# A selective scan behind two convolution blocks: softplus summed in PSUM, one odd product in five moved from GpSimd to VectorE, and the background work cut and paced anew

## The chip, the cores and the metric

One Trainium2 chip, one of its NeuronCores. Five engines run their own instruction streams in order and wait for each other by semaphores: TensorE (PE; its weight loads are PEld), VectorE (DVE), ScalarE (ACT), GpSimd (POOL) and SyncE (SP), which here only issues DMAs. SBUF is the on-chip memory of 128 partitions; PSUM holds what TensorE writes, eight banks of 128 x 512 fp32. The metric is the device time of one execution in microseconds.

## The reference

An image batch x of 16 x 64 x 64 x 96 (fp32) goes through two blocks, each with a group norm ahead and a residual. The first block upsamples by two in the Fourier domain, applies a 96-to-384 layer, a polynomial of second degree, a 384-to-96 layer, and low-passes back. The second is a selective scan in four directions, and the time goes there. Cut to what matters:

```
x = x + L0(gn(x))
x = x + L1(gn(x))
# inside L1, for each of 4 directions k, 192 channels d, 16 states n, 4096 places l:
delta = softplus(dts + bias)
h     = exp(delta * A) * h + (delta * u) * B
y     = sum over n of h * C   (+ u * Ds)
# then: layer norm of the four directions' sum, times silu(z), out projection
```

Softplus is computed as max(s, 0) + ln(1 + e) with e = exp(-|s|), and the rounding error of 1 + e is taken off: minus ((1 + e) - 1 - e).

## The kernel before, in words

`front(mi)` makes everything of image mi that comes ahead of the scan: its two norms, the first block (upsampling matmuls `u_ps`, `xu_ps`, the layers `h_ps`, `o_ps`, the way back `d_ps`, `e_ps`), then the 3 x 3 convolution `c_ps` with silu, with results written to DRAM (`xs`, `z`, `x1`). `finish(mi)` sums the directions after the scan, norms, gates and projects. `project` makes, for each step of 1024 places, the rows B and C and for three channel groups v delta = softplus(s) and dtu = delta * u, in pieces of 128 x 512, and writes them to DRAM. All three are Python generators; each `yield` ends a slice of work.

The scan is the main loop. It runs over 16 images, 8 steps per image (four chunks of 1024 places forward, four backward, two directions in each), 6 blocks of channels and 4 groups j of states: 3,072 positions n. A position works on 128 lanes (32 channels x 4 states) in two halves e = 1 ("odd") and e = 0 ("even"), each 128 x 1024:

- GpSimd `drive(n)`: b = dtu * B for both halves at once (128 x 2048, L725). `b` has three buffers, all in SBUF.
- ScalarE `decay(n, e)`: da = exp(delta * A) (L719). `da` lies in PSUM, two buffers, one for each half.
- VectorE `recur(n, e)`: the scan itself (L734 forward, L736 backward). The odd scan writes over its half of b, the even one over da in PSUM.
- ScalarE `keep(n, e)`: the last column, as the start of the next chunk (L742).
- The product of h with C: the odd half in place on GpSimd (L863, b and ct in SBUF), the even half on VectorE (L873, da in PSUM times ct in SBUF, into b).
- TensorE `read_out(n)`: sums over the states into the PSUM tile y (L758). `store` copies y out after each fourth position.

The order is written out by hand and is the order of every engine's stream. In position n: odd scan, `read_out(n - 1)`, a slot, `keep` and `decay(n + 1)` of the odd half, odd product, `drive(n + 2)`, even scan, a slot, even product, `keep` and `decay(n + 1)` of the even half, a slot. `drive(n + 2)` writes the buffer that `read_out(n - 1)` reads; the next odd product on GpSimd needs the next odd scan and the `keep` that reads its result.

In each `slot()` one slice of `project` for the next step is taken, and one of the background: `front` of the next image until it is done, then `finish` of the image before. `Background.slot` hands out SLICES = 404 slices in POS = 576 slots of an image, so about 0.70 per slot, whatever a slice holds.

Large transfers of `front` and `finish` (the image in, the way back `s`, `x1`, the turned `xs` out, `ycol` in: 7 per image of 0.75 to 2 MB) are issued on ScalarE's queue; all others, those for the scan among them, on SP's.

Of the kernel before, what the change touches and what calls it, by code (L numbers as in the profile page):

```python
# [51 lines left out]
C = 96  # L52
# [19 lines left out]
SLICES = 404  # L72
PSLICES = 60


@with_exitstack
def tile_two_blocks(
    ctx: ExitStack, tc: tile.TileContext,
    x, w1, w1t, b1, w2t, b2, coef, inpt, convw, convb, xpt, dtw, alog, dsk, onw, onb, opt,
# [31 lines left out]
    nc.gpsimd.memset(one_s, 1.0)  # L111
    eps_g = const.tile([128, 1], F32, name="eps_g")
# [79 lines left out]

    def norm(xt):
# [37 lines left out]
    def front(mi):  # L231

        x_c = x[mi].rearrange("h c w -> c h w")
# [7 lines left out]
        nc.scalar.dma_start(out=xt.rearrange("c (h w) -> c h w", w=HW), in_=x_c)  # L241
        for _ in range(4):
            yield
# [163 lines left out]
        for i, on in enumerate((slice(0, JS), slice(JS, HW))):  # L407
            nc.scalar.dma_start(out=s[i], in_=s_d[:, on, :])
        for _ in range(8):
            yield  # L410
        x1 = xt
# [19 lines left out]
        nc.scalar.dma_start(out=made["x1"], in_=x1)  # L431
# [13 lines left out]
        for i, n, tiles, both in ((0, 128, 8, 0), (1, 64, 4, 4)):  # L445
            col = b16.tile([128, tiles * TB], F32, name="col", tag="b16")
            parts = [(n * k, t0) for k, t0 in enumerate((0, both)[:128 // n])]
            turned = None

            def turn(t, row, z):  # L450
# [4 lines left out]
                for p, t0 in parts:  # L455
                    cols = slice(TB * (t + t0), TB * (t + t0) + TB)
                    nc.sync.dma_start(out=made["xs"][2 * i, 0:n, cols], in_=row[p:p + n])
                    nc.sync.dma_start(out=made["z"][128 * i:128 * i + n, cols], in_=z[p:p + n])

            for t in range(tiles):  # L460
                c_ps = bank([128, 8, HW], "c_ps")
                for tap in range(9):
                    dy, dx = divmod(tap, 3)
                    for p, t0 in parts:
# [8 lines left out]
                    if tap % 3 == 2 and tap < 8:  # L473
                        yield
                z_ps = bank([128, 8, HW], "z_ps")
                for p, t0 in parts:
# [5 lines left out]
                yield  # L482
# [5 lines left out]
                yield  # L488
            turn(*turned)
            yield  # L490
            if i == 0:
                nc.scalar.dma_start(out=made["xs"][1], in_=col)
            else:
                for p, t0 in parts:
                    to = made["xs"][2, 64:128, :].rearrange("c (w h) -> c w h", h=HW)
                    for w0 in range(0, HW, 16):
# [4 lines left out]
                        yield  # L501

    def finish(mi):
# [3 lines left out]
        nc.scalar.dma_start(out=ycol[0], in_=y_d[1, 0:128, :])  # L507
        nc.scalar.dma_start(out=ycol[1], in_=y_d[1, 128:DI, :])
# [11 lines left out]
        for _ in range(6):  # L520
            yield
        tail = None
        for t in range(8):
# [7 lines left out]
            for ob, n in ((0, 128), (1, 64)):  # L531
# [11 lines left out]
                yield  # L543
# [12 lines left out]
                yield  # L556
# [5 lines left out]
            yield  # L562
# [5 lines left out]
            yield  # L568
# [6 lines left out]
            yield  # L575
# [4 lines left out]
            yield  # L580
# [10 lines left out]
        for _ in tail:  # L591
            yield
# [6 lines left out]
    def scan():  # L599


        with ExitStack() as es:
# [12 lines left out]
            def project(mi, pair, lc, out):  # L615
# [7 lines left out]
                for t in range(0, T, TB):  # L623
# [15 lines left out]
                    for i, v in enumerate((0, 2, 1)):  # L639
# [10 lines left out]
                        e = pj.tile([128, TB], F32, name="e")  # L650
                        d = pj.tile([128, TB], F32, name="d")
                        nc.scalar.activation(e, s, AF.Abs)
                        nc.scalar.activation(e, e, AF.Exp, scale=-1.0)
                        yield
                        nc.scalar.activation(d, e, AF.Ln, bias=one_s)  # L655
                        yield
                        nc.vector.scalar_tensor_tensor(d, s, 0.0, d, ALU.max, ALU.add)  # L657
                        yield
                        nc.scalar.activation(s, e, AF.Identity, bias=one_s)
                        yield  # L660
                        nc.vector.scalar_tensor_tensor(s, s, -1.0, e, ALU.add, ALU.subtract)
                        nc.vector.tensor_sub(s, d, s)
                        yield
# [3 lines left out]
                        yield  # L667
# [118 lines left out]
            class Background:  # L786


                def __init__(self, gen, slices, positions):
                    self.gen, self.slices, self.positions, self.at, self.n = gen, slices, positions, 0, 0  # L790

                def slot(self):
                    self.at += 1
                    if self.gen is not None and self.n * self.positions < self.at * self.slices:
                        self.n += 1
                        if next(self.gen, 0) == 0:
                            self.gen = None

                def drain(self):
                    while self.gen is not None:  # L800
                        self.n += 1
                        if next(self.gen, 0) == 0:
                            self.gen = None
# [15 lines left out]
            for n, (st, bi, j) in enumerate(units):  # L819
# [11 lines left out]
                if j == 0:  # L831
                    if bi == 0 and st + 1 < len(steps):
                        if steps[st + 1][0] > mi:
                            ahead_gen.drain()
                        step_gen = Background(project(*steps[st + 1], ctxs[st + 1]), PSLICES, 58)
# [20 lines left out]
                recur(n, 1, h)  # L856
                if n:
                    read_out(n - 1)
                slot()
                keep(n, 1, h)  # L860
# [142 lines left out]
```

## Time and profile before

| | us |
|---|---|
| median of 3 runs | 22,337.41 (22,315.87 to 22,346.83) |
| the profiled execution | 22,310.87, span 22,309.1 |
| GpSimd busy | 20,896.4 (94%) |
| VectorE busy | 19,837.0 (89%) |
| TensorE busy, granted clock 0.74 on average | 15,814.4 (71%) |
| ScalarE busy | 13,129.1 (59%) |
| DMA queue of SP, share of 16 engines | 54.6% |
| DMA queue of ScalarE | 3.0% |

The groups on VectorE that the change touches:

```
L657 DVE SCALAR_TENSOR_TENSOR d<-s,d 128x512 x768 | 521.8, 679
L661 DVE SCALAR_TENSOR_TENSOR s<-s,e 128x512 x768 | 521.9, 680
L662 DVE TENSOR_TENSOR s<-d,s 128x512 x768 | 534.4, 696
L666 DVE TENSOR_TENSOR dtu<-s,u 128x512 x768 | 516.6, 673
```

A row is read so: source line, engine, operation, what it writes and reads, shape, how often; then the busy time of all in us and the mean of one in ns. (The rows here are cut after that.) A wait is put down to the instruction that came last. Where two records of an engine overlap by a few hundredths of a microsecond, the distance from start to start is what one instruction really takes of the engine's time.

### The profile page before, as it was taken

Reading aid. Unit: us, or ns where it says so; the run is one execution under the profiler, and the core shown is the slowest. Engines: PE = TensorE matmul, PEld = TensorE weight load, DVE = VectorE, ACT = ScalarE, POOL = GpSimd, SP = SyncE. Lnnn points to the kernel's source line nnn. Section 1 sums busy time; section 2 is a strip of 40 time slices with the busy share of each in tenths; the row PEclk is TensorE's granted clock in tenths of the full one; section 3 lists DMA queues with packets and bytes.
Section 4 is the critical chain, followed back from the end, with each engine's and each line's share of the span. In section 5 each row is a group of like instructions: output and inputs, shape, how many; then the busy total and the mean of one; then the engine's idle time right before and its main releaser. Section 6 shows DMA issues by size and latency. Waiting matters only on the chain.

```text
span 22309.1 us, 261027 instructions
## 1 busy us (share of the span) xinstructions
PE 15814.4 (71%) x92844; PEld 6455.6 (29%) x92844; DVE 19837.0 (89%) x12829; ACT 13129.1 (59%) x20854; POOL 20896.4 (94%) x6152
## 2 busy tenths in 40 slices
PE   6675777767778677776777777677786777767745
PEld 4322323223232322323223232332323223232211
DVE  0999999899998999989899898999989999898996
ACT  3665655656556565565656556565565655656543
POOL 0999999999999999999999999999999999999997
PEclk7676777877778677686777878677786776867856
DMA  2555565655656556565655656556565665656654
GB/s 77 185 194 184 191 210 182 209 191 193 206 189 210 184 198 204 190 210 186 203 194 191 210 184 209 192 189 209 189 212 184 201 201 190 210 186 203 211 177 133
DMA packets 1915769, 4276.30 MB, mean 192 GB/s; under 512 B 543454, under 2 KB 642686, under 8 KB 1906206
## 3 DMA queue, kind: packets, MB, share of 16 engines
q1 hardware_dynamic: 1804702, 4086.06, 54.6%
q10 hardware_dynamic: 109760, 173.55, 3.0%
q8 instruction: 731, 11.98, 0.2%
q14 instruction: 576, 4.72, 0.1%
HBM read 3380.58 MB, written 878.18 MB: 191 GB/s over the span
## 4 chain that ended last, share of the span: by engine, by line
POOL 31%; issue 20%; DVE 20%; PE 15%; DMA 8%; ACT 5%; SPq 1%; POOLq 0%; ACTq 0%; DVEq 0%
POOL b L863 15%; POOL b L725 15%; DVE da L736 4%; DVE b L734 4%; DVE da L734 4%; DVE b L736 3%; DVE b L873 3%; PE y L758 2%; PE c_ps L466 2%; DMA u<-xs_d 2%; PE pp L633 2%; ACT da L719 2%; PE yc L535 1%; DMA ct<-rows 1%; PE oe_ps L578 1%
## 5 line engine op out<-in xcount | busy, mean ns | idle before, releaser
L725 POOL TENSOR_TENSOR b<-dtu,bt 128x2048 f32<-128x2048 f32 x3072 | 14000.3, 4557 | 578.3 <-DMA dtu<-dtu_d 531.9
L758 PE MATMUL y<-b,fold_s 128*32 128x256 f32 x49152 | 4865.1, 506 | 4962.9 <-DVE b L873 3489.3
L719 ACT ACTIVATE da<-delta,a_s 128x1024 f32<-128x1024 f32 x6144 | 6855.9, 1116 | 2487.3 <-DVE b L873 1350.0
L863 POOL TENSOR_TENSOR b<-b,ct 128x1024 f32<-128x1024 f32 x3072 | 7323.1, 2384 | 668.3 <-ACT new L742 591.3
L758 PEld LDWEIGHTS y<-b,fold_s 128*32 128x32 f32 x49152 | 1324.5, 127 | 8709.7 <-DVE b L873 4353.2
L873 DVE TENSOR_TENSOR b<-da,ct 128x1024 f32<-128x1024 f32 x3072 | 3750.4, 1221 | 75.1
L736 DVE TENSOR_TENSOR_SCAN b<-da,new,b 128x1024 f32<-128x1024 f32 x1152 | 2697.2, 2341 | 376.5 <-ACT new L742 223.5
L734 DVE TENSOR_TENSOR_SCAN b<-da,new,b 128x1024 f32<-128x1024 f32 x1152 | 2700.9, 2344 | 288.4 <-POOL b L725 283.4
L736 DVE TENSOR_TENSOR_SCAN da<-da,new,b 128x1024 f32<-128x1024 f32 x1152 | 2692.7, 2337 | 108.4 <-ACT da L719 108.4
L734 DVE TENSOR_TENSOR_SCAN da<-da,new,b 128x1024 f32<-128x1024 f32 x1152 | 2693.5, 2338 | 85.3 <-ACT da L719 85.3
L742 ACT COPY new<-da 128x1 f32<-128x1 f32 x2304 | 362.6, 157 | 3347.7 <-DVE b L873 3344.4
L466 PE MATMUL c_ps<-xgp,wtap_s 96*128 96x512 f32 (+1 forms) x4608 | 1676.9, 625 | 119.1 <-ACT row L484 114.5
L643 PE MATMUL s<-pr,dtw_s 128*128 128x512 f32 x1536 | 1202.3, 875 | 244.6 <-ACT delta L668 212.5
L358 PE MATMUL h_ps<-xu,w1t_s 96*128 96x500 f32 x1920 | 1316.4, 798 | 74.3 <-ACT hsq L341 32.8
L633 PE MATMUL pp<-u,xpt_s 128*128 128x512 f32 x1536 | 1061.8, 844 | 372.9 <-DMA u<-xs_d 359.8
L370 PE MATMUL o_ps<-w2c_s,hsq 128*100 128x96 f32 x9600 | 1222.0, 296 | 25.8 <-ACT new L742 15.1
L370 PEld LDWEIGHTS o_ps<-w2c_s,hsq 128*100 128x100 f32 x9600 | 1154.6, 208 | 284.9 <-issue 186.6
L742 ACT COPY new<-b 128x1 f32<-128x1 f32 x2304 | 429.9, 187 | 1058.2 <-DVE b L734 587.7
L657 DVE SCALAR_TENSOR_TENSOR d<-s,d 128x512 f32<-128x512 f32 x768 | 521.8, 679 | 555.6 <-ACT d L655 553.1
L736 DVE TENSOR_TENSOR_SCAN da<-da,b 128x1024 f32<-128x1024 f32 x384 | 876.5, 2282 | 133.5 <-ACT da L719 133.5
L734 DVE TENSOR_TENSOR_SCAN b<-da,b 128x1024 f32<-128x1024 f32 x384 | 876.2, 2282 | 99.3 <-POOL b L725 65.7
L736 DVE TENSOR_TENSOR_SCAN b<-da,b 128x1024 f32<-128x1024 f32 x384 | 876.5, 2283 | 69.8 <-POOL b L725 65.5
(120 smaller groups left out, 18395.2 us busy)
## 6 DMA issues: line engine op xcount, KB each, us to landing
dtu<-dtu_d SPq DMA_DIRECT2D x1536, 512.0 KB
delta<-delta_d SPq DMA_DIRECT2D x1536, 512.0 KB
bt<-rows SPq DMA_DIRECT2D x1024, 512.0 KB
ct<-rows SPq DMA_DIRECT2D x1024, 512.0 KB
u<-xs_d SPq DMA_DIRECT2D x896, 256.0 KB
dtu_d<-dtu SPq DMA_DIRECT2D x768, 256.0 KB
delta_d<-delta SPq DMA_DIRECT2D x768, 256.0 KB
xr<-in_x SPq DMA_DIRECT2D x768, 128.0 KB
```

What stands on the lines that cost most here:

```text
L358: nc.tensor.matmul(h_ps[j], lhsT=w1t_s[:, 128 * j:128 * (j + 1)], rhs=xu.rearrange("c p q -> c (p q)"), start=True, stop=True,)
L370: nc.tensor.matmul(o_ps[:, p, :], lhsT=hsq[j][:, UPS * p:UPS * (p + 1)], rhs=w2c_s[:, j, :], start=(j == 0), stop=(j == HB - 1),)
L466: nc.tensor.matmul(c_ps[p:p + n], lhsT=wtap_s[:, tap, 128 * i:128 * i + n], rhs=xgp[:, h0:h0 + 8, dx:dx + HW], start=(tap == 0), stop=(tap ...
L633: nc.tensor.matmul(pp, lhsT=xpt_s[:, pair, v, :], rhs=u[v], start=(v == 0), stop=(v == 2))
L643: nc.tensor.matmul(s, lhsT=dtw_s[:, pair, v, :], rhs=pr, start=True, stop=True)
L719: nc.scalar.activation(da, ops["delta", n // NQ][:, e, :], AF.Exp, scale=a_s[:, k, g, units[n][2]:units[n][2] + 1])
L725: nc.gpsimd.tensor_mul(b, ops["dtu", n // NQ], bt.unsqueeze(1).to_broadcast([128, 2, T]))
L734: nc.vector.tensor_tensor_scan(out, da, b, before, ALU.mult, ALU.add)
L736: nc.vector.tensor_tensor_scan(out[:, ::-1], da[:, ::-1], b[:, ::-1], before, ALU.mult, ALU.add)
L758: nc.tensor.matmul(y[32 * q:32 * q + 32, e, :], lhsT=fold_s, rhs=b[:, e, QT * q:QT * q + QT], start=(pair == 0 and j == 0 and e == 0), sto ...
L863: nc.gpsimd.tensor_mul(h, h, bc[1, r, j])
L873: nc.vector.tensor_mul(bs[n][:, 0, :], h, bc[1, r, j])
```

## The change

Four things, in one diff.

1. Softplus. The three VectorE instructions and the ScalarE instruction that made max(s, 0) + ln(1 + e) and the correction are gone. ScalarE now writes m = max(s, 0) and w = (1 + e) - 1 into two new SBUF tiles, and TensorE adds -w + e + d + m in PSUM with four identity matmuls. The operands are made in the second and third slices after s, the sums in the fifth, and `dtu` and `delta` are read two slices after that.
2. Every fifth position (n % 5 == 4) has its odd product on VectorE, behind the even scan, instead of on GpSimd.
3. `keep` and `decay` of the odd half stand ahead of `read_out` and of the position's first slot.
4. The large transfers go to SP's queue in pieces with a `yield` after each, the image is read from a copy laid out by channels, and slices of the convolution and of `finish` count double (HEAVY) against SLICES = 540.

```diff
-SLICES = 404
+SLICES = 540
+HEAVY = 2
 PSLICES = 60
+SHARE = 5
...
+    less_s = const.tile([128, 1], F32, name="less_s")
+    nc.gpsimd.memset(less_s, -1.0)
+    less_i = const.tile([128, 128], F32, name="less_i")
+    nc.vector.tensor_scalar(less_i, ident_s, -1.0, None, ALU.mult)
...
+    def parts(out, in_, n=4):
+
+        step = L // n
+        for i in range(n):
+            nc.sync.dma_start(out=out[:, step * i:step * i + step], in_=in_[:, step * i:step * i + step])
+            yield
...
-        nc.scalar.dma_start(out=xt.rearrange("c (h w) -> c h w", w=HW), in_=x_c)
-        for _ in range(4):
-            yield
+        yield from parts(xt, xc[mi])
+        yield
...
-        for i, on in enumerate((slice(0, JS), slice(JS, HW))):
-            nc.scalar.dma_start(out=s[i], in_=s_d[:, on, :])
-        for _ in range(8):
+        for i, n, first in [(0, JS // 4, k * JS // 4) for k in range(4)] + [(1, 10, 0), (1, 10, 10)]:
+            nc.sync.dma_start(out=s[i][:, first:first + n, :], in_=s_d[:, JS * i + first:JS * i + first + n, :])
             yield
...
-        nc.scalar.dma_start(out=ycol[0], in_=y_d[1, 0:128, :])
-        nc.scalar.dma_start(out=ycol[1], in_=y_d[1, 128:DI, :])
+        yield from parts(ycol[0], y_d[1, 0:128, :])
+        yield from parts(ycol[1], y_d[1, 128:DI, :], 2)
...
-                        e = pj.tile([128, TB], F32, name="e")
-                        d = pj.tile([128, TB], F32, name="d")
+                        e, d, m, w = (pj.tile([128, TB], F32, name=k) for k in ("e", "d", "m", "w"))
                         nc.scalar.activation(e, s, AF.Abs)
                         nc.scalar.activation(e, e, AF.Exp, scale=-1.0)
                         yield
+                        nc.scalar.activation(m, s, AF.Relu)
+                        nc.scalar.activation(w, e, AF.Identity, bias=one_s)
+                        yield
                         nc.scalar.activation(d, e, AF.Ln, bias=one_s)
+                        nc.scalar.activation(w, w, AF.Identity, bias=less_s)
                         yield
-                        nc.vector.scalar_tensor_tensor(d, s, 0.0, d, ALU.max, ALU.add)
+                        s = gps.tile([128, TB], F32, name="s", tag="g")
                         yield
-                        nc.scalar.activation(s, e, AF.Identity, bias=one_s)
-                        yield
-                        nc.vector.scalar_tensor_tensor(s, s, -1.0, e, ALU.add, ALU.subtract)
-                        nc.vector.tensor_sub(s, d, s)
-                        yield
+                        for k, (sign, of) in enumerate(((less_i, w), (ident_s, e), (ident_s, d), (ident_s, m))):
+                            nc.tensor.matmul(s, lhsT=sign, rhs=of, start=(k == 0), stop=(k == 3))
+                        for _ in range(2):
+                            yield
...
                 def slot(self):
                     self.at += 1
                     if self.gen is not None and self.n * self.positions < self.at * self.slices:
-                        self.n += 1
-                        if next(self.gen, 0) == 0:
-                            self.gen = None
+                        self.step()
+
+                def step(self):
+                    weight = next(self.gen, 0)
+                    if weight == 0:
+                        self.gen = None
+                    else:
+                        self.n += weight or 1
...
                 h = bs[n][:, 1, :]
                 recur(n, 1, h)
+                keep(n, 1, h)
+                if n < last:
+                    decay(n + 1, 1)
                 if n:
                     read_out(n - 1)
                 slot()
-                keep(n, 1, h)
-                if n < last:
-                    decay(n + 1, 1)
-                nc.gpsimd.tensor_mul(h, h, bc[1, r, j])
+                odd_here = n % SHARE == SHARE - 1
+                if not odd_here:
+                    nc.gpsimd.tensor_mul(h, h, bc[1, r, j])
                 if n + 2 <= last:
                     drive(n + 2)
 
                 h = das[n, 0]
                 recur(n, 0, h)
+                if odd_here:
+                    nc.vector.tensor_mul(bs[n][:, 1, :], bs[n][:, 1, :], bc[1, r, j])
```

Left out of the diff above: the same split of `x1` and `xs`, the `yield HEAVY` in the convolution and in `finish` (whose six empty slices at the start become two heavy ones), a rename (`parts` to `halves`), and 59 in place of 58 as the slots over which `project` is spread.

## The prediction

> **What bounds the kernel now.** I read the groups of instructions first, then busy time by stretch, then the waits, then the order in time. The groups show GpSimd's two rows, `drive` (L725) and the odd product with C (L863), once per position:
>
> ```profile
> L725 POOL TENSOR_TENSOR b<-dtu,bt 128x2048 f32<-128x2048 f32 x3072 | 14000.3, 4557 | 578.3 <-DMA dtu<-dtu_d 531.9
> L863 POOL TENSOR_TENSOR b<-b,ct 128x1024 f32<-128x1024 f32 x3072 | 7323.1, 2384 | 668.3 <-ACT new L742 591.3
> ```
>
> Together 21,323 us in a span of 22,309.1 us. By stretch (columns: PE, PEld, DVE, ACT and POOL busy, granted clock, DMA share, GB/s):
>
> ```profile
> 1500.00:2500.00 1000.00, 629.86 (x4240) 260.56 (x4232) 932.12 (x587) 582.10 (x907) 990.79 (x292) 0.67 0.56 188
> 2500.00:3500.00 1000.00, 724.43 (x4000) 279.29 (x4000) 902.02 (x591) 607.60 (x979) 952.02 (x281) 0.77 0.62 203
> ```
>
> While the light first part of `front` runs behind the scan, GpSimd is never idle; in the second line (convolution and `finish`) it loses some 5%. The waits say to whom:
>
> ```profile
> POOL b L863 <- ACT new L742: 591.3, 229, 14.0
> ```
>
> That is `keep` coming late on ScalarE. The timeline gives the beat, and a warning:
>
> ```profile
> 4037.46 2.35 POOL L863 TENSOR_TENSOR b<-b,ct 128x1024 f32<-128x1024 f32 x1
> 4037.53 2.35 DVE L736 TENSOR_TENSOR_SCAN b<-da,new,b 128x1024 f32<-128x1024 f32 x1 [0.34 <-POOL b L725]
> 4039.78 4.52 POOL L725 TENSOR_TENSOR b<-dtu,bt 128x2048 f32<-128x2048 f32 x1
> 4039.79 2.33 DVE L736 TENSOR_TENSOR_SCAN da<-da,new,b 128x1024 f32<-128x1024 f32 x1
> ...
> 4042.16 1.23 DVE L873 TENSOR_TENSOR b<-da,ct 128x1024 f32<-128x1024 f32 x1
> ...
> 4046.56 4.50 POOL L725 TENSOR_TENSOR b<-dtu,bt 128x2048 f32<-128x2048 f32 x1
> ...
> 4048.84 9.00 DVE L227 TENSOR_TENSOR nb<-nmean,rg 96x1 f32<-96x1 f32 x1
> 4051.03 2.33 POOL L863 TENSOR_TENSOR b<-b,ct 128x1024 f32<-128x1024 f32 x1
> 4053.34 4.48 POOL L725 TENSOR_TENSOR b<-dtu,bt 128x2048 f32<-128x2048 f32 x1
> 4057.76 1.21 DVE L873 TENSOR_TENSOR b<-da,ct 128x1024 f32<-128x1024 f32 x1
> 4058.89 2.33 DVE L736 TENSOR_TENSOR_SCAN b<-da,new,b 128x1024 f32<-128x1024 f32 x1
> ...
> 4064.42 2.36 POOL L863 TENSOR_TENSOR b<-b,ct 128x1024 f32<-128x1024 f32 x1 [6.60 <-ACT new L742]
> ```
>
> From start to start GpSimd needs 2.31 us for the product and 4.47 to 4.49 for `drive`: 6.78 us per position. VectorE needs 2.26 (odd scan), 2.37 (even scan) and 1.13 (even product): 5.77 us. And `nb`, a product of 96x1 elements whose inputs both lie in SBUF, took 9.00 us: it ended only when GpSimd had nothing queued, and then GpSimd stood still for 6.60 us. Elsewhere it slipped in where one GpSimd instruction ended:
>
> ```profile
> 2698.13 4.51 POOL L725 TENSOR_TENSOR b<-dtu,bt 128x2048 f32<-128x2048 f32 x1
> ...
> 2700.40 2.25 DVE L227 TENSOR_TENSOR nb<-nmean,rg 96x1 f32<-96x1 f32 x1
> ...
> 2702.60 2.35 POOL L863 TENSOR_TENSOR b<-b,ct 128x1024 f32<-128x1024 f32 x1
> ```
>
> With GpSimd idle, before the scan, `nb` takes 0.155 us. Of the 31 `nb` and 15 `lin` (L252, 2.19 us against 0.245) that ran beside GpSimd, 41 ended at the next boundary and 5 missed two boundaries. All other VectorE products of the scan have one input in PSUM and never stretch (L873 1.22 us, L666 0.67).
>
> **The change part by part.**
> *Odd product on VectorE.* 614 of 3072 L863 go: 614 x 2.31 = 1,418 us off GpSimd, leaving 31.6 us for five positions (6.32 each). VectorE gets 614 x 1.13 = 694 us. But this product reads b and ct, both SBUF, beside `drive`: the form that waited in `nb`. Its wait is not in the trace for 1024 elements; below it is nothing (GpSimd idle), above the 9.00 us of `nb`. I walk five positions from time 0, where `drive` for the shared position ends. GpSimd runs the odd product of the position before until 2.3, the next `drive` until 6.78, and, with no product of its own, a further `drive` until 11.26. VectorE starts its odd scan at L (its lag) and reaches the product at L + 4.63.
> (a) L under 2.15 and the product wins the boundary: it runs 6.78 to 7.91, the `drive` behind it is pushed back 1.13, five positions cost 31.6 + 1.13 = 32.7 us: 6.55 each.
> (b) L over 2.15, or the boundary lost: the product waits until 11.26 and ends at 12.39, the even product at 13.53, the next odd scan at 15.80, `keep` and semaphores 0.35 more. GpSimd's next product needs that scan, so GpSimd stands still from 11.26 to 16.15, and five positions cost 16.15 + 3 x 6.78 = 36.5 us: 7.30 each, against the 7.03 of now ((22,309 - 532 - 167) / 3072; 532 us lie before the first `drive`, 167 after the last odd product).
> Which one holds is decided by the lag. After (a) VectorE stands at 7.91 + 1.14 + 4 x 5.77 = 32.1, that is 0.6 ahead of GpSimd; after (b) at 36.6, 0.1 behind; to both the remaining VectorE work and waits are added, next.
>
> *Softplus in PSUM.* VectorE loses L657, L661 and L662: 521.8 + 521.9 + 534.4 = 1,578 us. It was not the bound, so this buys only lag; `dtu` stays, 0.6 us apart, 6 times in 20 positions: 0.9 us in five. ScalarE loses L659 (519 us), gains a Relu (like L652, 586 ns) and two Identities (like L659, 676): 768 x 1.938 - 519 = +969 us on 13,129, off the path by itself. TensorE gains 768 x 4 matmuls of two instructions each. L583, the same identity with 96 rows, shows 596 ns; back to back they start 0.43 us apart at granted clock 0.99, at most 0.86 at half clock: 2,640 to 5,280 us on 15,814, hidden in its 29% idle and in a higher clock (20 us windows with TensorE 65% busy were granted 0.68, those above 90% 0.94). What it can cost is `dtu` waiting two slots later for the four sums: 0 to 2 us; I take 0.3 in five positions, since with VectorE lagging the sums are early.
>
> *`keep` and `decay` of the odd half before the slot.* Better for GpSimd (the 591 us above), worse for the even `decay`, which now has two slots' ScalarE work ahead of it instead of one. Counted in the order of both programs with the durations of the rows, light part: 0.75 us before, 1.67 after, and in 12 of 80 positions instead of none over the 2.8 us that there is room for (3.5 from the odd scan's end to the even product's, 2.26 of the next odd scan, less 1.55 and 1.4 for the two `keep` and `decay` pairs); the excess is 10 us in 80 positions; convolution 13 of 45 (23 us). Existing waits of VectorE for ScalarE in the light part are 11 us in 86 positions. Per five: 0.6 + 0.6 + 0.3 = 1.5 us light, some 3 in the convolution.
>
> *Pieces on SP and HEAVY.* The large ScalarE-queue transfers made u late and so ScalarE (in one case 15 us) and GpSimd (12.71). Of the 591 us I count most as gained, but in (b) GpSimd's new idle time covers it. Now 24 pieces per image queue on SP in front of u, dtu, delta; at some 0.5 us an issue that is 12 us per image, hidden as before. The light slices run at 540/576 per slot instead of 404/576, the heavy ones at half: same work, evenly laid. `project` still takes one piece per slot and is done after 58 of 72 slots; the two new constants cost one instruction each before the scan.
>
> *Sum.* Light: lag after (a) -0.6 + 0.9 + 1.5 = 1.8, after (b) 0.1 + 2.4 = 2.5: on either side of 2.15. I take 40% of (a): 7.0 us. Convolution, with 1.5 more, 15%: 7.2. `finish` adds 24 VectorE products of 0.6 in 46 positions (1.6 per five): (b) always, 7.3. By image 95 x 7.0 + 44 x 7.2 + 53 x 7.3 = 1,369 us, where `nb` to `nb` now shows 1,353. Fifteen images 20,535, the last (no `front`; 53 x 7.3 + 139 x 6.8) 1,332, head 532 + 22 (the first projection's sums in line: 2 to 5.6 us in each of six), tail 167: 22,590 us. The profiled execution (22,310.87) lies 27 below the median; I say 22,600.
>
> A rule against the change stands in the Trainium skill, SBUF — State Buffer, Who interferes with whom: a VectorE instruction with two SBUF inputs and a GpSimd instruction that reads SBUF exclude each other for their whole length, and issue order decides. The rows of `nb` agree on the exclusion, but five of them were overtaken twice; by the rule the product would win every boundary that it reaches in time, which makes the light part 6.9 and the total some 22,400.
>
> **The rivals.**
> 1. *The product nearly always in time* (lag kept small because 1,578 us left VectorE): for it, in the light part now only 16% of odd scans start over 2.15 us after their `drive`; against it, some 58% do in the heavy part. Light 6.6, convolution 6.75, `finish` 7.0: 1,295 per image, in all 15 x 1,295 + 1,281 + 721 = 21,430 us. It needs the remaining VectorE work and waits under 1.7 us in five positions. Faster.
> 2. *Always late*: 7.32 everywhere: 3072 x 7.32 + 721 = 23,200 us. For it: once in (b), the lag starts 0.7 higher.
> 3. *No exclusion at this size*: 6.32 plus some 0.25 of waits, 6.57 x 3072 + 721 = 20,900. The 46 stretched instructions speak against it.
> 4. TensorE as the bound: (15,814 + 5,280) / 3072 = 6.87 us at half clock, under 7.0; it could only add to 2.
>
> **How the numbers follow.** Forecast (mixture) 0.46, rival 1 0.30, rival 2 0.20, rival 3 0.04. The mixture's own range, with 20 to 60% of (a) in the light part, is 22,200 to 22,950. What a measurement of this kernel can tell from no change is 0.2%, 45 us. Faster: rivals 1 and 3 and a small part of the mixture, 0.36; same 0.05; slower 0.59. The range takes in rival 2 and most of rival 1: 21,300 to 23,300.
>
> **What would show it.** The new VectorE product's mean: 1.2 us without exclusion, about 2.5 in (a), 5 to 8 in (b); I expect 4 to 5. GpSimd idle before L863's successor some 4.9 us in (b), released by `keep` or the odd scan, every fifth position. L725's successor up to 1.1 us longer where the product went first. VectorE waiting for `da` more than now (482 us). I am wrong if the product's mean stays under 3 us, or if TensorE or a DMA releases GpSimd.

## The result, and the profile after

The changed kernel takes 23,058.78 us in the median of four runs (23,027.14 to 23,067.01), the kernel before 22,342.12 on the same chip: a ratio of 1.032, 95% interval 1.0302 to 1.0337. It is slower, as forecast, but by 3.2% and not by 1.2%. The profiled execution has a span of 23,025.1 us.

The engines' busy times (first part of the page) of the changed kernel:

```profile
PE 17468.4 (76%) x98988; PEld 7440.0 (32%) x98988; DVE 20342.6 (88%) x11140; ACT 13908.8 (60%) x22390; POOL 19763.7 (86%) x5539
```

GpSimd, 94% busy before, is at 86%; VectorE is now the busiest engine with 88%, and had 89% before. The groups of the scan (what is written from what, shape and count; busy us, mean ns; idle before, and what ended it):

```profile
L737 POOL TENSOR_TENSOR b<-dtu,bt 128x2048 f32<-128x2048 f32 x3072 | 14144.2, 4611 | 1214.8 <-DMA dtu<-dtu_d 552.9 <-PE y L770 370.9 <-issue 199.9
L881 POOL TENSOR_TENSOR b<-b,ct 128x1024 f32<-128x1024 f32 x2458 | 5795.8, 2358 | 1883.0 <-ACT new L754 1530.8 <-DVE b L746 193.9 <-DVE b L748 134.3
L893 DVE TENSOR_TENSOR b<-da,ct 128x1024 f32<-128x1024 f32 x3072 | 3748.1, 1220 | 74.0
L888 DVE TENSOR_TENSOR b<-b,ct 128x1024 f32<-128x1024 f32 x614 | 2070.0, 3371 | 19.7 <-ACT new L754 16.8 <-DMA xs_d<-row 2.9
```

The even product (L893, one input in PSUM) takes 1.22 us, the shared odd one (L888, both inputs in SBUF) 3.37 us on the same shape. GpSimd's idle time ahead of its own products (L881) has grown from 668.3 to 1,883.0 us. Two places show the two forms of L888. In the first, this is GpSimd and then VectorE in order of time (start, duration, and idle time before in brackets):

```profile
10041.51 10.06 POOL L737 TENSOR_TENSOR b<-dtu,bt 128x2048 f32<-128x2048 f32 x2
10051.53 2.35 POOL L881 TENSOR_TENSOR b<-b,ct 128x1024 f32<-128x1024 f32 x1
...
10043.75 2.33 DVE L748 TENSOR_TENSOR_SCAN da<-da,new,b 128x1024 f32<-128x1024 f32 x1
10045.99 1.20 DVE L888 TENSOR_TENSOR b<-b,ct 128x1024 f32<-128x1024 f32 x1
```

Two `drive`s in a row need 2 x 4.49 = 8.98 us; here they took 10.06, and the product's 1.20 us lie at the boundary between them. This is case (a). In the second place:

```profile
3383.39 8.98 POOL L737 TENSOR_TENSOR b<-dtu,bt 128x2048 f32<-128x2048 f32 x2
3397.09 2.35 POOL L881 TENSOR_TENSOR b<-b,ct 128x1024 f32<-128x1024 f32 x1 [4.72 <-ACT new L754]
...
3388.16 5.29 DVE L888 TENSOR_TENSOR b<-b,ct 128x1024 f32<-128x1024 f32 x1
3393.38 1.21 DVE L893 TENSOR_TENSOR b<-da,ct 128x1024 f32<-128x1024 f32 x1
3394.51 2.27 DVE L746 TENSOR_TENSOR_SCAN b<-da,b 128x1024 f32<-128x1024 f32 x1
```

The boundary lies at 3383.39 + 4.49 = 3387.88; the product came 0.28 us after it, waited for the whole second `drive` (to 3392.37) and ended 1.08 us behind it. VectorE's next odd scan came so much later, and GpSimd stood still for 4.72 us. This is case (b), as drawn in the prediction. A product that comes in time can lose the boundary too:

```profile
1084.36 9.00 POOL L737 TENSOR_TENSOR b<-dtu,bt 128x2048 f32<-128x2048 f32 x2
...
1086.64 7.80 DVE L888 TENSOR_TENSOR b<-b,ct 128x1024 f32<-128x1024 f32 x1
```

It began 2.2 us before the boundary and still ended behind the second `drive`. Of the 298 products that began more than 0.1 us ahead of it, 52 were passed over in this way.

GpSimd's idle time in (b) is there. What the prediction does not have is in VectorE's waits (waiting instruction, what it waited for, us, times, longest):

```profile
DVE dtu L679 <- PE s L674: 733.5, 320, 135.7
DVE da L746 <- ACT da L731: 631.3, 475, 6.1
DVE da L748 <- ACT da L731: 569.7, 354, 5.8
```

With two smaller rows for `decay` (55.8 and 27.3) these are 2,018 us; `da` alone has 1,284, where the kernel before had 486. And this is a stretch of 86 positions from the first part of image 2's scan, by busy time (PE, PEld, DVE, ACT, POOL, granted clock, DMA share, GB/s):

```profile
3323.00:3945.00 622.00, 481.14 (x3518) 255.50 (x3518) 564.46 (x300) 400.69 (x683) 553.04 (x155) 0.82 0.53 178
```

622 us for 86 positions are 36.2 us for five. GpSimd is idle for 69 us of it, VectorE for 57.5: both wait, in turn. VectorE's five positions add up so: 30.9 us of its own work (5 x 5.77 + 1.13 + 0.9 for `dtu`), some 2.2 by which L888 is stretched (3.37 less 1.2), and 3.1 of waits (34.8 us for `da` and 17 to 18 for `dtu` in 86 positions): 36.2. Over the first parts of 14 images the mean is 36.9, with 3.6 of these waits (2.4 for `da`, 1.3 for `dtu`).

By positions of an image (start to start of even products, mean of 14 images, us per position; the versions come in the next section):

| | 0 to 86 (light) | 86 to 131 (convolution) | 141 to 188 (`finish`) | whole image |
|---|---|---|---|---|
| before | 6.87 | 7.04 | 7.43 | 7.06 |
| forecast | 7.0 | 7.2 | 7.3 | 7.13 |
| after | 7.38 | 7.44 | 7.15 | 7.30 |
| e1, no share | 7.12 | 7.14 | 6.84 | 7.04 |
| e2, share with an operand in PSUM | 7.00 | 7.08 | 6.79 | 6.94 |
| e10, order, pieces and pace alone | 6.96 | 7.08 | 7.00 | 6.99 |
| e15, after with half the sums | 7.08 | 7.25 | 6.97 | 7.06 |
| e16, e2 with half the sums | 6.62 | 6.86 | 6.71 | 6.69 |

The names of the columns hold for the new pace. With the old one (before, and e7 below) the convolution's matmuls run at positions 125 to 148 and those of `finish` from 156 on, so there the columns are the same positions but not the same work. The expectations below quote some of these figures counted a few positions apart (7.39, 7.10, 6.8).

### The profile page after: what moved, and what is told of

The parts are those of the page before. It is cut to its first block, busy times and chain, and to the rows that moved or that the text cites. A ratio compares the mean times of both kernels' runs of the same rounds, so it can differ in the third digit from the quotient of the medians.

```text
span 23025.1 us, 273947 instructions
## 1 busy us (share of the span) xinstructions
PE 17468.4 (76%) x98988; PEld 7440.0 (32%) x98988; DVE 20342.6 (88%) x11140; ACT 13908.8 (60%) x22390; POOL 19763.7 (86%) x5539
## 5 line engine op out<-in xcount | busy, mean ns | idle before, releaser
L737 POOL TENSOR_TENSOR b<-dtu,bt 128x2048 f32<-128x2048 f32 x3072 | 14144.2, 4611 | 1214.8 <-DMA dtu<-dtu_d 552.9
L881 POOL TENSOR_TENSOR b<-b,ct 128x1024 f32<-128x1024 f32 x2458 | 5795.8, 2358 | 1883.0 <-ACT new L754 1530.8
L770 PE MATMUL y<-b,fold_s 128*32 128x256 f32 x49152 | 4067.6, 453 | 2916.4 <-DVE b L893 2685.2
L893 DVE TENSOR_TENSOR b<-da,ct 128x1024 f32<-128x1024 f32 x3072 | 3748.1, 1220 | 74.0
L770 PEld LDWEIGHTS y<-b,fold_s 128*32 128x32 f32 x49152 | 1403.7, 121 | 5815.2 <-DVE b L893 2647.9
L888 DVE TENSOR_TENSOR b<-b,ct 128x1024 f32<-128x1024 f32 x614 | 2070.0, 3371 | 19.7 <-ACT new L754 16.8
L674 PE MATMUL s<-w,less_i 128*128 128x512 f32 x1536 | 1228.8, 893 | 624.8 <-ACT w L669 623.4
L369 PE MATMUL h_ps<-xu,w1t_s 96*128 96x500 f32 x1920 | 1068.4, 655 | 170.4 <-ACT hsq L352 91.5
L654 PE MATMUL s<-pr,dtw_s 128*128 128x512 f32 x1536 | 917.7, 681 | 364.2 <-ACT delta L680 265.7
L679 DVE TENSOR_TENSOR dtu<-s,u 128x512 f32<-128x512 f32 x768 | 522.7, 681 | 746.6 <-PE s L674 733.5
L644 PE MATMUL pp<-u,xpt_s 128*128 128x512 f32 x1536 | 900.9, 728 | 283.7 <-DMA u<-xs_d 268.6
L674 PE MATMUL s<-e,ident_s 128*128 128x512 f32 x1536 | 1060.9, 782 | 0.0
```

The costliest lines, as they stand in the source:

```text
L369: nc.tensor.matmul(h_ps[j], lhsT=w1t_s[:, 128 * j:128 * (j + 1)], rhs=xu.rearrange("c p q -> c (p q)"), start=True, stop=True,)
L674: nc.tensor.matmul(s, lhsT=sign, rhs=of, start=(k == 0), stop=(k == 3))
L737: nc.gpsimd.tensor_mul(b, ops["dtu", n // NQ], bt.unsqueeze(1).to_broadcast([128, 2, T]))
L770: nc.tensor.matmul(y[32 * q:32 * q + 32, e, :], lhsT=fold_s, rhs=b[:, e, QT * q:QT * q + QT], start=(pair == 0 and j == 0 and e == 0), sto ...
L881: nc.gpsimd.tensor_mul(h, h, bc[1, r, j])
L888: nc.vector.tensor_mul(bs[n][:, 1, :], bs[n][:, 1, :], bc[1, r, j])
```

## The experiments

The kernel before ran beside every batch: medians of 22,329 to 22,335 us. Ratios are to it.

**What the share costs, and why.** e1 takes the share out of the changed kernel; e4 puts it, alone, into the kernel before.

```diff
-                odd_here = n % SHARE == SHARE - 1
+                odd_here = False
```

> The changed kernel with every odd product back on GpSimd. Theory 1 (the shared product, which waits for GpSimd on VectorE, costs the time): GpSimd is the bound again at 6.78 us per position in the light part, VectorE needs 5.77 + 0.2 for dtu + some 0.6 of waits and stays under it; GpSimd idle falls from 2,500 to some 500 us after its start, and the whole is 21,700 to 22,100 us, faster than before because the heavy parts lose less. Theory 2 (the sums on TensorE and the new order on ScalarE cost the time, by VectorE's waits for da and for the sums, 1,284 and 733 us in the changed kernel): the time stays over 22,700 us.

Measured: 22,277.82 us, 0.9977 (0.9967 to 0.9987). The share costs 23,059 - 22,278 = 781 us here; GpSimd's idle time for `keep` falls from 1,530.8 to 316.5. The time lies between the two theories, nearer the first. The light part stays at 7.12, above the 6.87 of before, so there a part of the loss has nothing to do with the share.

> The kernel before with one odd product in five on VectorE and nothing else changed. Theory 1: VectorE's five positions cost 5 x (5.77 + 0.6 for softplus) + 1.1 + some 2 of exclusion + 0.7 of waits = 35.6 us, 7.1 or more per position where before it was 6.8; the product's mean is 3 to 4 us and the whole 22,900 to 23,500 us, slower than before by more than 2%. Theory 2 (the other parts cost the time): 21,300 to 22,300 us, since 1,418 us leave GpSimd.

Measured: 23,569.79 us, 1.0554 (1.0537 to 1.0572): theory 1, 70 us above its range. The share costs 1,235 us in the kernel before; its product's mean is 3,432 ns.

Is it the place of the operands, or only that VectorE has more to do? e2 lets the shared position's odd scan write its result into `da`, in PSUM, instead of over b; the product then reads PSUM and SBUF. The next odd `decay` has to follow the product, since it writes that `da`. e9 is the same edit alone in the kernel before.

```diff
-                h = bs[n][:, 1, :]
+                odd_here = n % SHARE == SHARE - 1
+                h = das[n, 1] if odd_here else bs[n][:, 1, :]
                 recur(n, 1, h)
                 keep(n, 1, h)
-                if n < last:
+                if n < last and not odd_here:
                     decay(n + 1, 1)
...
+                h1, h = h, das[n, 0]
                 recur(n, 0, h)
                 if odd_here:
-                    nc.vector.tensor_mul(bs[n][:, 1, :], bs[n][:, 1, :], bc[1, r, j])
+                    nc.vector.tensor_mul(bs[n][:, 1, :], h1, bc[1, r, j])
+                    if n < last:
+                        decay(n + 1, 1)
```

> The changed kernel, but in every fifth position the odd scan writes over da in PSUM, so that the product on VectorE reads one operand from PSUM and one from SBUF; the next odd decay then waits for this product. Theory 1 (exclusion of two-SBUF-input products beside GpSimd): the product's mean falls from 3.37 to 1.22 us and GpSimd's idle time behind it shrinks; VectorE's five positions cost 31 + 3 of waits = 34 us or 6.8 per position in the light part instead of 7.39, the whole 21,500 to 22,100 us. Theory 2 (VectorE waits for ScalarE and TensorE whatever the product reads): mean 1.2 us too, but the time moves to waits for da, and the whole stays over 22,700 us.

Measured: 21,923.16 us, 0.9817 (0.9802 to 0.9831), 1,136 us less than the changed kernel 1.8% faster than the kernel before, with nothing left out, and in theory 1's range. The groups of e2 show the product:

```profile
L888 DVE TENSOR_TENSOR b<-da,ct 128x1024 f32<-128x1024 f32 x614 | 740.4, 1206 | 14.4 <-ACT new L754 14.4
```

Same engine, same place in the order, same size: 1,206 ns instead of 3,371.

> The kernel before with one odd product with C in five on VectorE, and nothing else of the change, but with that product's operand da written into PSUM by its scan, so that one of its two operands does not lie in SBUF. The same share with both operands in SBUF took 23,570 us against 22,335 us of the kernel before. T1 (the share costs because its product and GpSimd's operations keep each other waiting): without that, VectorE has 5 x 6.37 + 1.13 = 33.0 us and some 0.7 us of waits in five positions, 6.75 a position, against GpSimd's 6.6: 22,000 to 22,300 us, more than 1,200 us less than the share in SBUF. T2 (the share costs because VectorE is simply too full for it in the kernel before, whatever its operands): still above 23,200 us, with VectorE over 90% busy.

Measured: 22,470.8 us, 1.0059 (1.0042 to 1.0076). That is 1,099 us less than e4, so T2 falls; but it is 170 us above T1's range, VectorE being 91% busy and GpSimd waiting 1,557 us for `keep`. Here, with softplus still on VectorE, the share gains nothing even without its exclusion.

**Order.** e3 puts `keep` and `decay` of the odd half back behind the slot in the changed kernel, e5 does so in e2:

```diff
                 recur(n, 1, h)
-                keep(n, 1, h)
-                if n < last:
-                    decay(n + 1, 1)
                 if n:
                     read_out(n - 1)
                 slot()
+                keep(n, 1, h)
+                if n < last:
+                    decay(n + 1, 1)
```

> The changed kernel with keep and decay of the odd half behind the position's first slot again, as before. If the order makes the even decay late: VectorE's waits for da fall from 1,284 us to under 700, and the time falls by 150 to 600 us to 22,450 to 22,900. If the waits come from more work on ScalarE and TensorE whatever the order: waits for da stay over 1,000 us and the time within 100 us of 23,059; GpSimd waits more for keep in both cases.

Measured: 22,797.9 us, 1.0202 (1.0185 to 1.0219): the old order is 261 us better. The even scan's waits for `da` fall from 1,201 to 716 us:

```profile
DVE da L748 <- ACT da L731: 412.9, 219, 5.8
DVE da L746 <- ACT da L731: 302.7, 266, 2.1
```

All waits for `da` together are still 999 us, where the first theory had under 700, and GpSimd's for `keep` do not grow as expected (1,437, from 1,531).

> The kernel with the product from PSUM (21,923 us), with keep and decay of the odd half behind the position's first slot as before the change. If the order makes the even decay late: 200 to 350 us less, 21,580 to 21,720 us, and VectorE's waits for da in the even scans (1,209 us) roughly halved, as in the changed kernel, where they fell from 1,201 to 716. If without the exclusion the order no longer matters: within 60 us of 21,923.

Measured: 21,949.1 us, 0.9832 (0.9817 to 0.9847). The waits for `da` fall here too (1,209 to 838), those of GpSimd for `keep` rise (895 to 1,165), and nothing is gained, as the second theory had it: the order costs 261 us beside the exclusion and nothing measurable without it.

**Softplus and pace.** e6 is e2 with the old softplus, e10 the changed kernel with neither the share nor the new softplus, so the order, the DMA pieces and the pace alone. e6's edit, which e10 combines with e1's:

```diff
-                        nc.scalar.activation(m, s, AF.Relu)
-                        nc.scalar.activation(w, e, AF.Identity, bias=one_s)
-                        yield
...
-                        for k, (sign, of) in enumerate(((less_i, w), (ident_s, e), (ident_s, d), (ident_s, m))):
-                            nc.tensor.matmul(s, lhsT=sign, rhs=of, start=(k == 0), stop=(k == 3))
+                        nc.vector.scalar_tensor_tensor(d, s, 0.0, d, ALU.max, ALU.add)
...
+                        nc.vector.scalar_tensor_tensor(s, s, -1.0, e, ALU.add, ALU.subtract)
+                        nc.vector.tensor_sub(s, d, s)
```

> The kernel with the product from PSUM, with softplus made on VectorE and ScalarE as before (1,578 us back on VectorE, 6,144 matmul instructions and two of three ScalarE instructions less). If the sums' waits (807 us for dtu, and da made late by the fuller ScalarE) outweigh what left VectorE: at or under 21,900 us. If VectorE's own work counts: 5 x (5.77 + 0.6) + 1.1 + 1 = 34 us in five positions where the sums leave 30.9 and their waits; 22,000 to 22,400 us.

Measured: 22,313.81 us, 0.9991 (0.9982 to 1.0). The new softplus is worth 391 us in e2, as the second theory had it, though VectorE's waits for `da` are 1,209 us with it (the rows of the even scan) and 416 without:

```profile
DVE da L747 <- ACT da L730: 220.5, 166, 6.0
DVE da L745 <- ACT da L730: 195.7, 134, 5.5
```

> The changed kernel without the shared product and with the old softplus on VectorE: what is left of the change is the order of decay and keep, the slices' even pacing and the small DMA pieces. The changed kernel without the share alone took 22,278 us, 7.10 us a position in the first part of a step. T1 (the sums in PSUM fill ScalarE and TensorE, and so cause VectorE's waits for da and dtu there): without them the first part falls to 6.9 or less and the whole to 21,700 to 21,950 us. T2 (the even pacing makes the first part longer, whichever way softplus is computed): 22,200 us or more, with 7.1 a position there.

Measured: 22,123.27 us, 0.9904 (0.989 to 0.9919): between the two, and so is the light part, at 6.96. Against e1 the new softplus makes the kernel 155 us slower where GpSimd is the bound; against e6 it makes it 391 us faster where VectorE is. Order, pieces and pace together gain 210 us on the kernel before.

e7 gives e2 the old density of slices, e12 one half way (480 and 1.5):

```diff
-SLICES = 540
-HEAVY = 2
+SLICES = 416
+HEAVY = 1
```

> The kernel with the product from PSUM, with every background slice counting one and 416 slices in 576 slots (0.72 per slot for all, where the light ones had 0.94 and the heavy ones 0.47). If the density of the light slices on ScalarE and TensorE makes the light part 7.0 us per position: it falls to 6.7 or less there and waits for da fall; convolution and finish rise to 7.3 or more, the whole 21,700 to 21,950 us. If density does not matter: light part stays at 7.0 us and the whole within 100 us of 21,923 or above.

Measured: 22,329.14 us, 1.0 (0.999 to 1.001): the new pace is worth 406 us in e2. Positions 0 to 86 fall to 6.76 and 141 to 188 rise to 7.62. The first theory has the direction of both, but the whole is 380 us above its range.

> The version with the shared product's operand in PSUM (21,923 us), with a pace of slices half way between the old and the new: 480 slices' worth and weight 1.5 in place of the changed kernel's. T1 (the pace only trades the first part of a step against its last): the first part falls from 7.00 to about 6.87 a position, the last rises from 6.63 to about 7.1, and the whole stays within 100 us of 21,923 us. T2 (there is a best pace between the two, since each part has slack to a point): more than 100 us below 21,923 us.

Measured: 21,910.49 us, 0.9808 (0.9791 to 0.9824): 6.84 in the light part, 7.03 in the last, the whole within 13 us of e2. T1: between these densities the pace trades one part against another.

**VectorE's waits.** e8 puts `dtu` three slots behind the sums instead of two; e11 does the same by issuing the sums one slot earlier.

```diff
-                        for _ in range(2):
+                        for _ in range(3):
```

> The kernel with the product from PSUM, with dtu and delta read three slots after the sums are issued instead of two. If VectorE loses time because the sums are not done two slots later: its waits for them fall from 807 us (136 of them before the scan) to under 400 and the time by 150 to 350 us. If those waits only take the place of waits for da: time within 60 us of 21,923.

Measured: 22,398.73 us, 1.0029 (1.0019 to 1.0039), with waits at `dtu` of 1,214 us in only 191 places. It does not tell what it was meant to: `project` then has 64 slices, PSLICES counts on 60, and the last ones are run all at once.

> The version with the shared product's operand in PSUM (21,923 us), with the softplus sums issued one slot earlier, so that dtu stands three slots behind the last of them instead of two; the number of slices is the same. T1 (VectorE's waits at dtu, some 800 us, are for sums that TensorE and ScalarE finish late): waits at dtu under 450 us, and the whole 100 to 300 us less. T2 (the waits only move: the sums then wait for their own projections, and VectorE for decay): within 60 us of 21,923 us, with waits for da that grow by what those at dtu lose.

Measured: 22,050.82 us, 0.9872 (0.9857 to 0.9887), 128 us more than e2. The waits at `dtu` fall to 409 us as T1 has it, but those for `da` rise by some 300, and neither range holds. Where the time went shows in TensorE's row for the first of the four sums, in e2 and in e11:

```profile
L674 PE MATMUL s<-w,less_i 128*128 128x512 f32 x1536 | 1193.0, 869 | 638.2 <-ACT w L669 633.8 <-ACT new L754 4.0
```

```profile
L673 PE MATMUL s<-w,less_i 128*128 128x512 f32 x1536 | 1253.6, 910 | 1493.3 <-ACT w L669 1106.1 <-ACT new L753 385.9
```

TensorE stands still ahead of the sums for 638 us in e2, nearly all of it for ScalarE's w, and for 1,493 when they are issued earlier (1,106 for w, 386 for `keep`). All that is queued behind on TensorE, `read_out` among it, stands too: in e11 GpSimd waits 478 us for y (358 in e2). So the waits are not a matter of the place alone. That left the amount of work, and e13 to e16 take it away: e13 two of the four matmuls (only d + m is summed), e14 the two Identity instructions on ScalarE (the first matmul reads e in place of w), e16 both; e15 is both in the changed kernel itself, with the product in SBUF.

```diff
-                        nc.scalar.activation(w, e, AF.Identity, bias=one_s)
...
-                        nc.scalar.activation(w, w, AF.Identity, bias=less_s)
...
-                        for k, (sign, of) in enumerate(((less_i, w), (ident_s, e), (ident_s, d), (ident_s, m))):
-                            nc.tensor.matmul(s, lhsT=sign, rhs=of, start=(k == 0), stop=(k == 3))
+                        for k, (sign, of) in enumerate(((ident_s, d), (ident_s, m))):
+                            nc.tensor.matmul(s, lhsT=sign, rhs=of, start=(k == 0), stop=(k == 1))
```

> The version with the shared product's operand in PSUM (21,923 us), with two of the four matmuls of each softplus sum left out: d + m alone is summed, the rounding term is not computed on TensorE; ScalarE's work is unchanged. T1 (TensorE, busy 78% in that version, makes the sums and with them dtu late): waits at dtu fall from 807 us to under 500, and the whole by 150 us or more, to 21,770 or less. T2 (ScalarE's added instructions are what VectorE waits for): within 60 us of 21,923 us, waits for da unchanged at about 1,300 us.

Measured: 21,482.38 us, 0.9619 (0.9603 to 0.9635): 441 us less than e2, waits at `dtu` 366 us. T1; the waits for `da` fall a little too, from 1,311 to 1,226.

> The same version with the two Identity instructions on ScalarE left out that make w for each softplus piece (the first matmul of the sum reads e in its place, so the rounding term cancels and TensorE's work is unchanged): 1,536 instructions of some 0.68 us, 1,040 us of ScalarE's 13,905. T1 (ScalarE's instructions ahead of decay are what VectorE waits for): waits for da fall from about 1,310 us to under 900, and the whole by 150 us or more, to 21,770 or less. T2 (TensorE's sums are what is late): within 60 us of 21,923 us.

Measured: 21,579.06 us, 0.9662 (0.9648 to 0.9677): 344 us less. T1 in the time; the waits for `da` fall only from 1,311 to 1,042. TensorE's row in e14 says where else it helped:

```profile
L672 PE MATMUL s<-e,less_i 128*128 128x512 f32 x1536 | 1114.8, 816 | 74.0 <-ACT m L665 73.9
```

The 638 us before the first sum are down to 74. e13 and e14 each named the other's engine as the alternative; both engines count.

> The version with the shared product's operand in PSUM (21,923 us), with both left out at once: the two Identity instructions and two of the four matmuls of each softplus piece. T1 (VectorE's waits for TensorE and ScalarE are what stands between 21,923 us and the 20,900 to 21,400 us that the engines' own work would allow): 21,300 to 21,650 us, the gains of the two single removals or more. T2 (the waits come from the order and the pace, not from the amount of work): above 21,800 us.

Measured: 21,158.22 us, 0.9474 (0.946 to 0.9488): 765 us less than e2, against 441 + 344 = 785 for the two apart: T1, 142 us below its range.

> The changed kernel itself (23,059 us), shared product with both operands in SBUF, with both left out: the two Identity instructions and two of the four matmuls of each softplus piece, so the rounding term is missing from delta. It takes from ScalarE and TensorE most of what the new softplus added, and leaves VectorE's and GpSimd's work as it is. T1 (the forecast's exclusion was right and its term for VectorE's waits too small): VectorE's waits at dtu and da fall from 2,017 us to 1,300 or less, the first part of a step from 7.39 us a position to 7.0 to 7.15, and the whole to 22,400 to 22,750 us, where the forecast stood. T2 (the exclusion sets the cycle, and VectorE's waits only fill it): 22,900 us or more, with the products no shorter than 3.3 us in the mean.

Measured: 22,321.64 us, 0.9996 (0.9986 to 1.0006): 737 us less than the changed kernel, 78 below T1's range, with the light part at 7.08 where it expected 7.0 to 7.15. Its waits and its product:

```profile
DVE da L744 <- ACT da L729: 459.9, 321, 6.1
DVE da L746 <- ACT da L729: 408.9, 301, 6.1
DVE nb L240 <- ACT rg L237: 297.2, 2, 276.8
DVE dtu L677 <- PE s L672: 292.2, 98, 133.3
DVE b L746 <- POOL b L735: 61.8, 65, 3.5
DVE b L746 <- ACT da L729: 40.3, 32, 1.5
```

```profile
L886 DVE TENSOR_TENSOR b<-b,ct 128x1024 f32<-128x1024 f32 x614 | 2172.1, 3538 | 16.2 <-ACT new L752 16.1
```

VectorE's waits at `da` and `dtu` are 1,228 us instead of 2,018 (one further row of 26.8 included), and the time follows, though the product is as long as ever: T2 falls.

## Why the prediction came out as it did

**Direction and mechanism.** The exclusion is as the prediction had it. Three pairs that differ in where the product's operand lies, and with it in the place of one `decay`, price it: 23,059 - 21,923 = 1,136 us, 23,570 - 22,471 = 1,099, 22,322 - 21,158 = 1,163, some 1.8 us for each shared position. The Trainium skill, page SBUF — State Buffer, section Who interferes with whom, says that a VectorE instruction with at most one SBUF input, outside the modes that use both ports, does not contend with GpSimd; the 1,206 ns of e2 agree. What the prediction calls the rule, that the product wins every boundary that it reaches in time, does not hold here: 52 of 298 lost it.

**Which case.** The product's mean is 3.4 us where 4 to 5 was expected: it is early 44% of the time in the light part, about as chosen (40%), 44% in the convolution (15% taken), and 66% in `finish` (never, by the prediction). Late means GpSimd idle for over 2 us behind it, 4.9 to 5.1 on average; the late products take 4.4 to 5.3 us, the early ones some 2.1. Cut as the prediction cuts it, from the end of the shared position's `drive` to the end of the `drive` five positions on, a light cycle takes 35.0 us when the product is early and 38.1 when it is late, where 32.7 and 36.5 were forecast. The order of the two cases is right, and each is longer than its price.

Rival 2, always late, comes nearest in time, 23,200 against 23,059, but by luck: half of the products are early. Two errors of the forecast also cancel in part. Without the exclusion it had 20,900 us (rival 3), and e2 takes 21,923: 1,023 too little. The exclusion, priced by the step from there to 22,600 at 1,700 us, costs 1,136 between e2 and the changed kernel: 564 too much. The 459 us that are left are the distance from 22,600 to 23,059.

**The step that failed** is the term for VectorE's waits in "Softplus in PSUM". ScalarE's extra work was taken as "off the path by itself", TensorE's as "hidden in its 29% idle", and what it can cost was put at "0.3 in five positions", since "with VectorE lagging the sums are early". With the order's 0.6 and the existing 0.6 this made 1.5 us of VectorE waits per five positions in the light part. Measured are 3.6 (1.3 at `dtu`, 2.4 at `da`; 3.1 in the stretch of image 2). So the light part went to 7.38 and not 7.0: VectorE, with 30.9 of work, 2.2 of stretch and these waits, needs some 36.9 for five positions, and neither case keeps its price. The order's 0.6 was about right: with the old order (e3) the waits are 0.8 less. e2 and e6 differ in softplus alone, and there the even scan's waits for `da` in the light part are 2.4 and 0.7. e15 shows that this is the term: with two matmuls and two ScalarE instructions per piece taken away and the exclusion left as it is, the light part is 7.08, the two cases take 33.7 and 37.0, and the whole is 22,322 us, within the mixture's own range of 22,200 to 22,950. Put at 0.3 for each of 614 cycles, all the sums would cost 184 us; taking half of them away gave back 737. Rival 3's case errs on the same side: no exclusion at all (e2) is 21,923 us, not 20,900, and 21,158 (e16) with half the sums.

Idle time did not cover the work, because TensorE and ScalarE run in order between the scan's own instructions. In the changed kernel TensorE waited 625 us at the head of the sums for w:

```profile
L674 PE MATMUL s<-w,less_i 128*128 128x512 f32 x1536 | 1228.8, 893 | 624.8 <-ACT w L669 623.4 <-ACT new L754 1.2
L674 PE MATMUL s<-e,ident_s 128*128 128x512 f32 x1536 | 1060.9, 782 | 0.0
L674 PE MATMUL s<-d,ident_s 128*128 128x512 f32 x1536 | 889.2, 663 | 0.0
L674 PE MATMUL s<-m,ident_s 128*128 128x512 f32 x1536 | 798.0, 601 | 0.0
```

`dtu` reads these sums, and `da` stands in ScalarE's order behind the instructions that make w. That taking either away gains time (e13 and e14) fits this; how the loss is shared between the two engines stays open. The busy share of an engine says nothing of it. The matmuls' own price was inside its bounds: the four groups of L674 are busy 1,229 + 1,061 + 889 + 798 = 3,977 us, forecast 2,640 to 5,280.

**Order.** Counted as a gain for GpSimd and 0.6 us per five for VectorE. In the changed kernel it is a loss of 261 us: GpSimd's wait for `keep`, which it was to shorten, is 1,531 us with it and 1,437 without, and VectorE's for `da` are longer.

**Pieces and pace.** Taken as the same work evenly laid. With the order they gain 210 us (e10): a whole image takes 6.99 us per position against 7.06. This offset a part of the miss: `finish` was forecast at 7.3, and is 7.15 with the share.

**Head and tail.** The first `drive` waits 543 us for dtu (543.2 of the 552.9 in the DMA row), against 532 + 22 forecast.

**Readings of the kernel before.** Thirty `nb` ran beside GpSimd and not 31, some 20% of the light part's odd scans start over 2.15 us after their `drive` and not 16%, and VectorE's waits for `da` are 486 us and not 482. None of this moves the sum.

**Open.** Why a product that begins ahead of the boundary is sometimes passed over is not shown; and e8 does not tell what a `dtu` further back alone would bring.

## What to carry to other kernels

Before moving an elementwise product from GpSimd to VectorE, look where its two inputs lie: with both in SBUF the move took 3.4 us a product and lost 781 us (e1 against the changed kernel), with one in PSUM it took 1.2 and gained 355 (e1 against e2). It gained only where softplus had left VectorE: with the old softplus it lost some 190 (e10 against e6). Work put on an engine with idle time isn't free where that engine feeds the bound in order: count what stands behind the first new instruction that can wait, and who waits for that. Of the full versions, e2 and e12 are the fastest, 1.8 and 1.9% under the kernel before; e16, without the rounding term, is 5.3% under it.

## What the runs showed of the hardware

Both sides pay at a boundary: in the first place above an early product lengthened two `drive`s by 1.08 us, and `drive`'s mean is 4,611 ns in the changed kernel against 4,535 in e2. The granted TensorE clock rose from 0.74 to 0.825 with more work on TensorE (71% to 76% busy), and stands at 0.757 in e10 without the sums; `read_out`'s matmuls took 453 ns in the mean in the changed kernel (L770) and 506 before (L758). So a part of TensorE's added work came back as clock.
